# Four heads in 32-row tiles of TensorE, float32 numerators and two-bank tiles in the third stage of a four-stage kernel

## The chip, the cores and the metric

The kernel runs on one core of a Trainium2 chip. The metric is the device time of one execution in microseconds (us). The kernel has some 28,000 instructions on TensorE (PE), VectorE (DVE), ScalarE (ACT), GpSimd (POOL) and the DMA queues that SyncE (SP) issues.

## The reference, cut to what matters

Four sublayers follow one another on x of 2 x 1024 tokens of 128 features: an attention without a mask, a routed feed-forward network, a causal attention with linear position biases (the third stage, the one that is changed), and two layers of local attention with a feed-forward network. Each is added to x after a layer normalisation of its input and of its output. The third one:

```python
B, S, D, H = (2, 1024, 128, 16)            # S as x has it
HD = D // H                                # 8 features per head
q = (x @ Wq + bq).reshape(Bb, Ss, H, HD)   # k and v the same way
scores = jnp.einsum('bthd,bshd->bhts', q, k) / jnp.sqrt(jnp.asarray(HD, x.dtype))
alibi = slopes[:, None, None] * -jnp.abs(kpos - qpos)[None]
scores = scores + alibi[None]
scores = jnp.where(causal[None, None], -jnp.inf, scores)
attn = jax.nn.softmax(scores, axis=-1)
out = jnp.einsum('bhts,bshd->bthd', attn, v).reshape(Bb, Ss, Dd)
return out @ Wo + bo
```

## The kernel before, in words

**Stages.** The functions phase1 to phase4 are the four sublayers. A scheduler that simulates the engines orders the instructions of each engine, within what the data allow. Two things fix more than that. `in_line` (L129) chains the TensorE instructions of successive calls, so that PE executes them in the order of the program. And `tick` (L1541) lets the next stage prepare itself (load weights, make tables) behind instructions that are named to it.

**The third stage's units.** Two batches and four groups of four heads make eight groups (u = 0 to 7), of twelve steps each (`order`, L881). A step takes 128 keys (j) and a half of 512 queries (c): four steps for the first half, of widths 512, 384, 256 and 128, then eight for the second half, widths 512 four times without a mask and then 512, 384, 256, 128. A diagonal block is masked by one more matmul, the identity times a causal matrix in bfloat16 (L864, L897).

**q and k of a group (`make`, L821).** Both are kept as one stack of 128 rows in float16, so that a product of one pass has the precision of a split: rows 0 to 95 hold the 32 projected features (4 heads of 8) three times, as high part, low part and high part in the order that makes the wanted cross products; rows 96 to 127 hold constants for the position bias and, in q, the negated maximum of each query. A projection is 2 x 3 matmuls (`mm3`, L47, high and low parts); ACT evicts the high part, DVE subtracts for the low part, and a DMA brings the 32 constant rows. Since all four heads lie in the same 128 rows, k is spread into four copies `kz`, one per head, each with the other heads' rows multiplied by zero (four `tensor_scalar` of 128 x 1024; from the second group on two of them on POOL).

**Maxima (`max_pass`, L853, and `max_rows`, L871).** For each tile of 128 queries and each half of keys the products of all four heads are formed in PSUM, and DVE reduces them to negated maxima (L869). For four tiles at a time the maxima are transposed by four matmuls (L878) into rows 96 to 127 of q (copy L879 on ACT), so that the score product afterwards gives score minus maximum.

**Scores and values (`scores`, L883, and `values`, L906).** A product per head (L895), its mask (L897), and an exponent on ACT (L898) into float32 numerators `pt`. On even steps the numerators are split further into float16 high and low parts: a copy on ACT (L902) and a subtraction on POOL (L903), 128 x 4w each. Their product with the values (L920) accumulates in one PSUM bank, a column tile of 32 per head; on even steps it is float16 twice (low part, then high part), on odd steps once in float32.

**Output (`outputs`, L933, and `finish`, L952).** After each half of queries a matmul with a constant matrix (L942) brings the sums into token order, with normalisation on DVE. After a batch's last group the output projection and the layer normalisation follow.

**PSUM.** `bank` (L786) hands out single banks of 128 x 512 float32, alternately from two rings of three (`bankz` and `bank`); near the end only the latter is used, as the other is handed to the next stage. One unit of maxima or one product of 512 columns takes one bank.

**Order of the loop (L966 to L1003).** A step m issues in this order: the scores of step m, the pending update of the maximum rows, the values of step m-4, the maxima for the group that lies 12 steps ahead (38 reductions per group, spread over the steps), a projection of q or k for the next group in steps 3 and 5, and the outputs of step m-5. From m = 54 on each step ends with a tick for stage 4's preparation, which hangs on the newest exponent, reduction, DMA and `kz` product.

Of the kernel before, what the change touches and what calls it, by code (L numbers as in the profile page):

```python
# [22 lines left out]
NT = N // 128  # L23
# [681 lines left out]
def phase3(k, X):  # L705
# [5 lines left out]
    with ExitStack() as es:  # L711
# [10 lines left out]
        pick = cp.tile([128, 4], F32, name="pick")  # L722
        nc.sync.dma_start(pick, A["c_pick3"])
        both = cp.tile([128, G * (HD + 1)], F32, name="both")
        nc.sync.dma_start(both, A["c_both3"])
        bias = cp.tile([96, 2, G], F32, name="bias")
# [7 lines left out]
        for i, n in enumerate("qk"):  # L734
            w = work().rearrange("p t d -> p (t d)")[:, : G * 96].rearrange("p (g m) -> p g m", g=G)
            nc.sync.dma_start(w, A["t_wqk3"][:, i])
            h = cp.tile([128, G, 96], F32R, name=n + "wh")
            l = cp.tile([128, G, 96], F32R, name=n + "wl")
            if n == "q":
                nc.vector.tensor_scalar(w, w, scale, None, ALU.mult)  # L740
            k.split_r(h, l, w)
            wqk[n] = h, l
            yield
# [37 lines left out]
        pz = es.enter_context(k.psum("p3z", 3))  # L781
        pb = es.enter_context(k.psum("p3b", 3))
# [3 lines left out]
        def bank():  # L786

            turn[0] += 1
            other = turn[0] * 3 % 6 < 3 and not turn[1]
            return pz.tile([128, 512], F32, name="bankz") if other else pb.tile([128, 512], F32, name="bank")  # L790


        of = (vp, wp)
        V = [of[i].tile([128, NT, 16, HD + 1], F32, name=f"V{i}") for i in range(2)]

        V16 = [of[i].tile([128, NT, 16, 32], F16, name=f"W{i}") for i in range(2)]
        mx = wp.tile([128, G, NT, 32], F16, name="mx")
        nc.sync.dma_start(mx, A["c_mx3"])
        mx2 = wp.tile([128, 2, 4, 4], F16, name="mx2")
        ao = [k.acc, wp.tile([128, NT, D], F32, name="ao")]  # L800
        for i in range(2):
            nc.gpsimd.memset(V[i][:, :, :, HD : HD + 1], 1.0)
            nc.gpsimd.memset(V16[i][:, :, :, HD:32], 0.0)
            nc.gpsimd.memset(V16[i][:, :, :, HD : HD + 1], 1.0)

        def values_of(b):
            xTh, xTl = S["x", b]
            for c in range(2):
# [7 lines left out]
                v, h = V[b][:, 4 * c : 4 * c + 4, :, 0:HD], V16[b][:, 4 * c : 4 * c + 4]  # L816
                nc.scalar.copy(h[:, :, :, 0:HD], v)
                nc.gpsimd.tensor_tensor(h[:, :, :, HD + 1 : 2 * HD + 1], v, h[:, :, :, 0:HD], ALU.subtract)
                yield

        def make(u, n):  # L821
            b, g = u // G, u % G
            xTh, xTl = S["x", b]
            wh, wl = wqk[n]
            i = 0 if n == "q" else 1
            stk = qp.tile([128, N], F16, name=n + "st", bufs=3 if n == "q" else 1)
            S["dma"] = nc.sync.dma_start(stk[96:128, :], A["c_rows3"][i, g])
            bc = bias[:, i, g : g + 1]
            lo = slice(32, 64) if n == "q" else slice(64, 96)
            for c in range(2):  # L830
                s = slice(512 * c, 512 * c + 512)
                ps = bank()
                k.mm3(ps[:96, :], wh[:, g, :], wl[:, g, :], xTh[:, s], xTl[:, s])
                nc.scalar.activation(stk[:96, s], ps[:96, :], AF.Identity, bias=bc)
                nc.vector.scalar_tensor_tensor(stk[lo, s], ps[lo, :], bc[lo, :], stk[lo, s], ALU.add, ALU.subtract)
            if n == "k":
                kz = qp.tile([128, 4, N], F16, name="kz")
                for a in range(4):
                    if u and a < 2:
                        S["kz"] = nc.gpsimd.tensor_scalar(kz[:, a, :], stk, pick[:, a : a + 1], None, ALU.mult)  # L840
                    else:
                        nc.vector.tensor_scalar(kz[:, a, :], stk, pick[:, a : a + 1], None, ALU.mult)
                stk = kz
            S[n, u] = stk


        units = []
        for t in range(NT):
            for e in range(t // 4 + 1):
                m = {1: 4, 2: 2}.get(t + 1 - 4 * e, 1)  # L850
                units += [(t, e, a, m) for a in range(0, 4, m)]

        def max_pass(u, i):  # L853
            t, e, a0, m = units[i]
            n = 128 * min(4, t + 1 - 4 * e)
            ps = bank().rearrange("p (a n) -> p a n", a=m)
            q0, kz = S["q", u], S["k", u]
            diag = e == t // 4
            for a in range(m):
                nc.tensor.matmul(  # L860
                    ps[:, a, :n], q0[:, 128 * t : 128 * t + 128], kz[:, a0 + a, 512 * e : 512 * e + n], start=True, stop=not diag
                )
                if diag:
                    nc.tensor.matmul(ps[:, a, n - 128 : n], identb, causal[:, 0, :], start=False, stop=True)  # L864
            if e == 0:
                out = mx[:, u % G, t, :].rearrange("p (a r) -> p a r", r=8)[:, a0 : a0 + m, 6]
            else:
                out = mx2[:, u % 2, t - 4, a0 : a0 + m]
            S["max"] = nc.vector.tensor_reduce(out, ps[:, :, :n], AX.X, ALU.max, negate=True)  # L869

        def max_rows(u, c):  # L871
            if c:
                m = mx[:, u % G, 4:8, :].rearrange("p t (a r) -> p t a r", r=8)[:, :, :, 6]
                nc.vector.tensor_tensor(m, m, mx2[:, u % 2, :, :], ALU.min)
            ps = bank()
            for t in range(4 * c, 4 * c + 4):
                s = slice(128 * (t % 4), 128 * (t % 4) + 128)
                nc.tensor.matmul(ps[96:128, s], mx[:, u % G, t, :], k.ident16, start=True, stop=True, tile_position=(0, 96))  # L878
            nc.scalar.copy(S["q", u][96:128, 512 * c : 512 * c + 512], ps[96:128, :])  # L879
# [3 lines left out]
        def scores(n):  # L883
            u = n // 12
            c, j = order[n % 12]
            q1, kz = S["q", u], S["k", u]
            s = max(512 * c, 128 * j)
            w = 512 * c + 512 - s
            diag = j >= 4 * c
            pt = pp.tile([128, 4, 512], F32, name="pt")  # L890
            m = {128: 4, 256: 2}.get(w, 1)
            for a0 in range(0, 4, m):
                st = bank().rearrange("p (a n) -> p a n", a=m)
                for a in range(m):
                    nc.tensor.matmul(st[:, a, :w], kz[:, a0 + a, 128 * j : 128 * j + 128], q1[:, s : s + w], start=True, stop=not diag)  # L895
                    if diag:
                        nc.tensor.matmul(st[:, a, :128], identb, causal[:, 1, :], start=False, stop=True)  # L897
                S["exp"] = nc.scalar.activation(pt[:, a0 : a0 + m, :w], st[:, :, :w], AF.Exp)  # L898
            hl = None
            if n % 2 == 0:  # L900
                hl = pp.tile([128, 2, 4, 512], F16, name="hl", bufs=2)
                nc.scalar.copy(hl[:, 0, :, :w], pt[:, :, :w])  # L902
                nc.gpsimd.tensor_tensor(hl[:, 1, :, :w], pt[:, :, :w], hl[:, 0, :, :w], ALU.subtract)  # L903
            S["p", n] = pt, hl, s, w

        def values(n):  # L906
# [6 lines left out]
            pt, hl, s, w = S.pop(("p", n))  # L913

            parts = [(V[b], lambda a: pt[:, a, :w])]
            if hl is not None:
                parts = [(V16[b], lambda a, i=i: hl[:, i, a, :w]) for i in (1, 0)]
            for i, (v, of_head) in enumerate(parts):
                for a in reversed(range(4)):
                    nc.tensor.matmul(  # L920
                        po[32 * a : 32 * a + v.shape[3], s - 512 * c : 512],
                        v[:, j, 4 * g + a, :],
                        of_head(a),
                        start=j == 0 and i == 0,
                        stop=j == 4 * c + 3 and i == len(parts) - 1,
                        tile_position=(0, 32 * a),
                    )
# [5 lines left out]
        def outputs(n):  # L933
# [7 lines left out]
            for i in range(4):  # L941
                nc.tensor.matmul(ps[:, i, :, :], ot[:, 128 * i : 128 * i + 128], both, start=True, stop=True)  # L942
# [9 lines left out]
        def finish(b, c):  # L952
# [6 lines left out]
            ps = bank().rearrange("p (t d) -> p t d", d=D)  # L959
# [8 lines left out]
        todo = [(u, i) for u in range(groups) for i in range(len(units))]  # L968
        half = [t for t, *_ in units].index(4) - 1
        ahead = 12  # L970
        for n in "qk":
            make(0, n)
        done = 0
# [3 lines left out]
        for m in range(-ahead, steps + 8):  # L977
# [4 lines left out]
            turn[1] = int(m >= steps - 14)  # L982
            if 0 <= m < steps:
                put(scores, m)
            u = m + ahead
# [3 lines left out]
            rows = [(u // 12 - 1, 1)] if u % 12 == 0 and 12 <= u < steps + 12 else []  # L989
            if 0 <= m - 4 < steps:  # L990
                put(values, m - 4)
            while done < len(todo) and done < (u + 1) * len(units) / 12:
# [685 lines left out]
```

## Time and profile before

| what | value |
|---|---|
| runs | 1356.66, 1354.52, 1354.22 us (median 1354.52) |
| the profiled execution's own time | 1356.68 us |
| its span in the trace | 1354.9 us |
| granted TensorE clock, mean | 0.945 |
| stage 3: first projection, first scores, last scores, last output | 600.6, 640.9, 954.1, 980.4 us |
| reductions of the maxima on DVE, L869 (two groups) | 304 x 0.65 us, 198.7 us busy |
| exponents on ACT, L898 (two groups) | 304 x 0.58 us, 173.8 us busy |
| subtraction on POOL, L903 | 48 x 3.43 us, 164.4 us busy |

The page begins with the busy time of each engine over the whole span; those are means over four stages with different limits. A stretch view gives the same for parts of the span. The timeline of one engine has a line per run of equal instructions: start in us, duration of one (or, for several, of the run), engine, line, the program's names (output<-inputs), shapes, type and count. A wait stands behind in brackets with the engine and line that ended it. The other 1.8 us of the profiled execution lie around its span.

### The profile page before, as it was taken

How to read it: one execution, taken by the hardware profiler on the slowest of the kernel's cores; microseconds unless marked ns; L12 is line 12 of the kernel's file. 1: busy time of each engine (PE TensorE's matmuls, PEld its weight loads, DVE VectorE, ACT ScalarE, POOL GpSimd, SP SyncE). 2: the span in 40 equal slices, each digit the busy share in tenths (PEclk: the TensorE clock that was granted, in tenths of full speed). 3: DMA queues.
4: the chain of work that ended last, by engine and by line, in shares of the span. 5: the costliest groups of instructions: out<-in, count | busy, mean ns of one | idle time of the engine just before them, and what ended most of it. 6: DMA issues, size and time to landing. Idle time of an engine off the chain costs nothing.

```text
span 1354.9 us, 28455 instructions
## 1 busy us (share of the span) xinstructions
PE 1162.4 (86%) x11558; PEld 716.5 (53%) x11558; DVE 982.3 (72%) x1970; ACT 958.2 (71%) x1481; POOL 842.6 (62%) x525
## 2 busy tenths in 40 slices
PE   4799999999897889887799998798668898998886
PEld 1366666666565646443355544343336565666564
DVE  6777666776674385989888789571578887888855
ACT  2777777787686364541898987789367788887755
POOL 1666667777665463733676768785577886666611
PEclk8899999999898999998999999898679899999999
DMA  2000000000000031300000013000157666555520
GB/s 77 1 2 2 2 2 1 2 17 18 1 1 2 18 131 32 112 13 4 3 5 3 5 38 73 1 21 1 24 94 163 122 119 106 103 99 100 106 59 16
DMA packets 123394, 57.59 MB, mean 43 GB/s; under 512 B 105568, under 2 KB 114800, under 8 KB 123264
## 3 DMA queue, kind: packets, MB, share of 16 engines
q1 hardware_dynamic: 121360, 54.50, 18.7%
q8 instruction: 90, 1.47, 0.4%
q10 hardware_dynamic: 1472, 1.09, 0.3%
q0 software_dynamic: 432, 0.20, 0.2%
q14 instruction: 40, 0.33, 0.1%
HBM read 21.69 MB, written 1.11 MB: 17 GB/s over the span
## 4 chain that ended last, share of the span: by engine, by line
PE 42%; DVE 29%; ACT 14%; issue 6%; POOL 4%; DMA 3%; SPq 0%; POOLq 0%; DVEq 0%; ACTq 0%
DVE mx L869 5%; PE big L360 5%; PE pu L49 4%; PE pu L51 3%; PE pu L50 3%; DVE nm L332 3%; PE pu L920 3%; ACT pt L898 2%; PE big L49 2%; PE big L51 2%; PE big L50 2%; PE bank L895 1%; PE bank L860 1%; PE big L656 1%; DVE ln_st L81 1%
## 5 line engine op out<-in xcount | busy, mean ns | idle before, releaser
L367 POOL TENSOR_TENSOR hl<-p,hl 128x1024 f16<-128x1024 f32 x128 | 274.0, 2143 | 142.8 <-ACT hl L366 116.2
L903 POOL TENSOR_TENSOR hl<-pt,hl 128x2048 f16<-128x2048 f32 (+1 forms) x48 | 164.4, 3432 | 78.1 <-ACT hl L902 68.4
L332 DVE TENSOR_REDUCE nm<-big 128x2 f32<-128x1024 f32 x128 | 155.2, 1220 | 32.3 <-PE big L329 31.6
L364 ACT ACTIVATE p<-big 128x1024 f32<-128x1024 f32 x128 | 130.9, 1023 | 52.4 <-PE big L360 51.6
L49 PEld LDWEIGHTS <-hl 128*128 128x128 f16 x1024 | 100.5, 98 | 75.7 <-DVE acc L392 43.6
L366 ACT CAST hl<-p 128x1024 f16<-128x1024 f32 x128 | 133.8, 1045 | 4.1
L869 DVE TENSOR_REDUCE mx<-bank 128x1 f16<-128x512 f32 (+3 forms) x157 | 102.1, 653 | 32.1 <-PE bank L860 16.4
L869 DVE TENSOR_REDUCE mx<-bankz 128x1 f16<-128x512 f32 (+3 forms) x147 | 96.6, 660 | 18.7 <-PE bankz L864 12.8
L898 ACT ACTIVATE pt<-bank 128x512 f32<-128x512 f32 (+1 forms) x172 | 97.0, 582 | 18.5 <-PE bank L897 11.1
L49 PE MATMUL pu<-V1h,hl 128*128 128x129 f16 x512 | 92.6, 224 | 12.4 <-DVE acc L392 11.7
L49 PE MATMUL pu<-V0h,hl 128*128 128x129 f16 x512 | 93.1, 224 | 10.8 <-DVE acc L392 9.5
L50 PEld LDWEIGHTS <-hl 128*128 128x128 f16 x1024 | 101.3, 99 | 0.0
L1221 POOL TENSOR_TENSOR rot<-rot,rn 128x512 f32<-128x512 f32 x64 | 66.3, 1056 | 55.8 <-DVE rn L1211 50.4
L51 PEld LDWEIGHTS <-hl 128*128 128x128 f16 x1024 | 100.5, 98 | 0.0
L1196 POOL TENSOR_TENSOR rot<-rot,t 128x512 f32<-128x512 f32 x64 | 84.1, 1326 | 20.2 <-DVE t L1190 20.1
L51 PE MATMUL pu<-V0h,hl 128*128 128x129 f16 x512 | 92.5, 223 | 0.0
L50 PE MATMUL pu<-V0l,hl 128*128 128x129 f16 x512 | 92.5, 222 | 0.0
L51 PE MATMUL pu<-V1h,hl 128*128 128x129 f16 x512 | 92.0, 222 | 0.0
L50 PE MATMUL pu<-V1l,hl 128*128 128x129 f16 x512 | 92.0, 221 | 0.0
L898 ACT ACTIVATE pt<-bankz 128x512 f32<-128x512 f32 (+1 forms) x132 | 76.8, 583 | 20.8 <-PE bankz L897 9.9
L88 POOL TENSOR_TENSOR ln_rstd<-ln_rs,nhalf 128x4 f32<-128x4 f32 (+2 forms) x29 | 32.8, 1135 | 81.4 <-DVE ln_rs L84 67.3
L895 PE MATMUL bank<-qst,kz 128*128 128x512 f16 (+3 forms) x218 | 68.1, 345 | 13.5 <-DVE mx L869 7.5
(412 smaller groups left out, 3730.9 us busy)
## 6 DMA issues: line engine op xcount, KB each, us to landing
sb<-sd SPq DMA_DIRECT2D x16, 512.0 KB, 4.4
Vs<-V SPq DMA_DIRECT2D x60, 130.0 KB, 2.4
work<-in_t_w SPq DMA_DIRECT2D x2, 512.0 KB, 3.5
out<-F SPq DMA_DIRECT2D x3, 256.0 KB, 2.3
X<-in_L_attn_x SPq DMA_DIRECT2D x2, 256.0 KB, 3.3
w<-in_t_wqk SPq DMA_DIRECT2D x1, 512.0 KB, 5.1
wv<-in_t_wv ACTq DMA_DIRECT2D x1, 512.0 KB
X<-in_L_attn_x ACTq DMA_DIRECT2D x1, 512.0 KB, 5.0
```

The costliest lines, as they stand in the source:

```text
L49: mm(out, lh, rh, start=start, stop=False, **kw)
L50: mm(out, lh, rl, start=False, stop=False, **kw)
L51: mm(out, ll, rh, start=False, stop=stop, **kw)
L332: S["red"] = nc.vector.tensor_reduce(S["n", u][:, i // 2, c, :], ps, AX.X, ALU.max, negate=True)
L364: S["exp"] = nc.scalar.activation(p, st, AF.Exp, scale=QSCALE**-2)
L366: nc.scalar.copy(hl[:, 0], p)
L367: S["lo"] = nc.gpsimd.tensor_tensor(hl[:, 1], p, hl[:, 0], ALU.subtract)
L869: S["max"] = nc.vector.tensor_reduce(out, ps[:, :, :n], AX.X, ALU.max, negate=True)
L895: nc.tensor.matmul(st[:, a, :w], kz[:, a0 + a, 128 * j : 128 * j + 128], q1[:, s : s + w], start=True, stop=not diag)
L898: S["exp"] = nc.scalar.activation(pt[:, a0 : a0 + m, :w], st[:, :, :w], AF.Exp)
L903: nc.gpsimd.tensor_tensor(hl[:, 1, :, :w], pt[:, :, :w], hl[:, 0, :, :w], ALU.subtract)
L1196: eng("ra" if j else "rb", i).tensor_tensor(rot[:, j], rot[:, j], t2[:, j], ALU.add)
```

## The change

The four heads' rows no longer lie together by kind; each head's rows lie together in 32 partitions: its 8 features three times, then 8 rows of constants. The weights are laid out for that (t_wqk3 has 128 columns per group). `make` projects both halves into one two-bank tile, ACT copies the sum whole to float32 `t`, a multiplication with a column of zeros and ones (`low`) makes `hi`, a subtraction makes the stack (both on POOL, in the first group on DVE), and four DMAs, issued after that, bring each head's 8 constant rows. The spread `kz` and its products are gone.

`products` multiplies four heads: two per pair of banks, each from its own 32 rows (`tile_position`), followed by the masks of the two, full-height matmuls. The pairs come from one ring of three. A unit of maxima is now all four heads, two pairs and two reductions; there are 12 units per group, one per step. `max_rows` copies the whole half of q by a product with the identity, adds the maxima to it in four more matmuls, and copies the result back over q on ACT. The numerators are used in float32 in all steps; the copy L902, the subtraction L903 and the second values product are gone, and the float32 values are 32 wide. The loop keeps the maxima 10 steps ahead rather than 12, the values 2 steps late rather than 4 and the outputs 3 rather than 5; the update of the second half's rows comes in the step after its last maxima, where it came one step later.

```diff
-        pz = es.enter_context(k.psum("p3z", 3))
-        pb = es.enter_context(k.psum("p3b", 3))
+        pz = es.enter_context(k.psum("p3z", 1))
+        pb = es.enter_context(k.psum("p3b", 2))
...
+        def pair():
+            turn[0] += 1
+            if turn[0] % 3 == 1 and not turn[1]:
+                return pz.tile([128, 2, 512], F32, name="pairz")
+            return pb.tile([128, 2, 512], F32, name="pair")
...
         def make(u, n):
...
+            ps = pair()
             for c in range(2):
                 s = slice(512 * c, 512 * c + 512)
...
+                k.mm3(ps[:, c, :], wh[:, g, :], wl[:, g, :], xTh[:, s], xTl[:, s])
+            t = qp.tile([128, N], F32, name="t", bufs=2)
+            nc.scalar.activation(t, ps.rearrange("p c n -> p (c n)"), AF.Identity, bias=bias[:, i, g : g + 1])
+            hi = qp.tile([128, N], F16, name="hi", bufs=1)
+            stk = qp.tile([128, N], F16, name=n + "st")
+            eng = nc.gpsimd if u else nc.vector
+            eng.tensor_scalar(hi, t, low[:, i : i + 1], None, ALU.mult)
+            S["stk"] = eng.tensor_tensor(stk, t, hi, ALU.subtract)
+            for a in range(4):
+                S["dma"] = nc.sync.dma_start(stk[32 * a + 24 : 32 * a + 32, :], A["c_rows3"][i, g, a])
             S[n, u] = stk
...
+        row = lambda a: slice(32 * a, 32 * a + 32)
+        def products(l, r, w, mask=None, at=0):
+            for a0 in (0, 2):
+                ps = pair()
+                for e in range(2):
+                    d = row(a0 + e)
+                    nc.tensor.matmul(ps[:, e, :w], l[d, :], r[d, :], start=True, stop=mask is None, tile_position=(d.start, 0))
+                for e in range(2 if mask is not None else 0):
+                    nc.tensor.matmul(ps[:, e, at : at + 128], identb, mask, start=False, stop=True)
+                yield slice(a0, a0 + 2), ps[:, :, :w]
+        units = [(t, e) for t in range(NT) for e in range(t // 4 + 1)]
         def max_pass(u, i):
...
+            for a, ps in products(q0[:, 128 * t : 128 * t + 128], kst[:, 512 * e : 512 * e + n], n, mask, n - 128):
+                S["max"] = nc.vector.tensor_reduce(out[:, a], ps, AX.X, ALU.max, negate=True)
         def max_rows(u, c):
...
+            ps = pair()[:, 0, :]
+            q = S["q", u][:, 512 * c : 512 * c + 512]
+            nc.tensor.matmul(ps, k.ident16, q, start=True, stop=False)
+            for i in range(4):
+                nc.tensor.matmul(ps[:, 128 * i : 128 * i + 128], mx[u % 2][:, 4 * c + i, :], k.ident16, start=False, stop=i == 3)
+            nc.scalar.copy(q, ps)
         def scores(n):
...
+            for a, ps in products(kst[:, 128 * j : 128 * j + 128], q1[:, s : s + w], w, mask):
+                S["exp"] = nc.scalar.activation(pt[:, a, :w], ps, AF.Exp)
-                hl = pp.tile([128, 2, 4, 512], F16, name="hl", bufs=2)
-                nc.scalar.copy(hl[:, 0, :, :w], pt[:, :, :w])
-                nc.gpsimd.tensor_tensor(hl[:, 1, :, :w], pt[:, :, :w], hl[:, 0, :, :w], ALU.subtract)
         def values(n):
...
+            for a in reversed(range(4)):
+                nc.tensor.matmul(po[32 * a : 32 * a + 32, s - 512 * c : 512], V[b][:, j, 4 * g + a, :],
+                    pt[:, a, :w], start=j == 0, stop=j == 4 * c + 3, tile_position=(0, 32 * a))
...
+        ahead, lag = 10, 2
+        for m in range(-ahead, steps + lag + 4):
...
+            turn[1] = int(m >= steps - 8)
             if 0 <= m < steps:
                 put(scores, m)
             for unit in rows:
                 put(max_rows, *unit)
+            rows = []
+            if 0 <= m - lag < steps:
+                put(values, m - lag)
+            u, i = (m + ahead) // 12, (m + ahead) % 12
+            if u < groups:
+                put(max_pass, u, i)
+                if i in (half, 11):
+                    rows.append((u, int(i == 11)))
+                if i in (3, 5) and u + 1 < groups:
+                    put(make, u + 1, "q" if i == 3 else "k")
             ends[:] = [e for e in ends if put(next, e, 0) is None]
+            if 0 <= m - lag - 1 < steps:
+                put(outputs, m - lag - 1)
             if m >= 54:
+                k.tick(S["exp"], S["max"], S["dma"], S["stk"])
```

## The prediction, made before the changed kernel ran

> **What bounds it now.** I read the page's totals first, then the busy time in stretches, then the order of TensorE's work in one group of stage 3, then who waited in its slowest stretch.
>
> ```profile
> span 1354.9 us, 28455 instructions
> ...
> PE 1162.4 (86%) x11558; PEld 716.5 (53%) x11558; DVE 982.3 (72%) x1970; ACT 958.2 (71%) x1481; POOL 842.6 (62%) x525
> ```
>
> These are means over four stages, so I price the change in stage 3 alone. In the stretches (busy us and count of PE, PEld, DVE, ACT, POOL, then the granted clock, the DMA share and GB/s):
>
> ```profile
> 600.00:641.00 41.00, 27.95 (x141) 15.60 (x142) 38.76 (x94) 6.51 (x10) 14.84 (x9) 0.88 0.03 7
> ...
> 746.16:781.77 35.61, 33.95 (x294) 17.23 (x293) 27.72 (x50) 32.90 (x53) 26.15 (x9) 1.00 0.02 6
> ...
> 866.00:886.00 20.00, 13.55 (x96) 6.02 (x95) 7.67 (x15) 10.02 (x17) 19.92 (x11) 0.83 0.00 1
> ...
> 921.00:955.00 34.00, 28.68 (x197) 12.29 (x198) 1.42 (x6) 29.49 (x48) 18.36 (x5) 0.75 0.00 1
> 955.00:981.00 26.00, 13.19 (x78) 9.14 (x71) 17.59 (x52) 7.42 (x17) 12.61 (x18) 0.58 0.20 31
> ```
>
> Before 641 DVE is the limit. The second row is one undisturbed group of twelve steps: PE is 95% busy, ACT 92%. At 866 POOL never rests and PE starves; at 921, where no maxima are left, ACT leads. From TensorE's timeline the scores of step 0 of groups 0 to 7 begin at 640.9, 682.3, 719.7, 757.0, 794.4, 835.1, 884.9 and 920.9, and the last step at 954.1. Durations that I need (start, us):
>
> ```profile
> 750.49 0.22 PE L897 MATMUL bank<-causal,identb 128*128 128x128 bf16 x1
> 750.63 1.05 PE L920 MATMUL pu<-pt,V 128*9 128x512 f32 x8
> 751.62 0.34 PE L860 MATMUL bankz<-kz,qst 128*128 128x384 f16 x1
> ...
> 758.06 0.22 PE L897 MATMUL bank<-causal,identb 128*128 128x128 bf16 x1
> 758.21 0.61 PE L920 MATMUL pu<-hl,W 128*32 128x512 f16 x8
> 758.76 0.23 PE L860 MATMUL bankz<-kz,qst 128*128 128x128 f16 x1
> ```
>
> Start to start, float32 values of 512 columns hold PE for 0.99 us, the split ones for 0.55. A mask takes 0.055; the 0.15 from mask to values shows some 0.09 lost when the tiling changes. Stage 1 has the nearest thing to the new products, two 64-row tiles:
>
> ```profile
> 150.59 0.39 PE L360 MATMUL big<-qh,kh 64*128 64x512 f16 x2
> 150.82 0.38 PE L360 MATMUL big<-ql,kh 64*128 64x512 f16 x2
> ...
> 154.68 0.38 PE L329 MATMUL big<-kh,qh 64*128 64x512 f16 x2
> 154.99 0.23 PE L49 MATMUL pu<-V1h,hl 128*128 128x129 f16 x1
> ```
>
> Both of a pair pass in 0.21 to 0.23 us, the time of one; 0.31 at the change to 128 rows again shows about 0.1 for the switch. The large evictions are these:
>
> ```profile
> L332 DVE TENSOR_REDUCE nm<-big 128x2 f32<-128x1024 f32 x128 | 155.2, 1220 | 32.3 <-PE big L329 31.6
> L364 ACT ACTIVATE p<-big 128x1024 f32<-128x1024 f32 x128 | 130.9, 1023 | 52.4 <-PE big L360 51.6
> ```
>
> **TensorE's work does not shrink.** Per group, scores and maxima each have 4608 columns of four heads. Before: 72 x 0.217 = 15.6 us, 64 masks 3.5, values 4 x 0.55 + 2 x 0.34 + 2 x 0.99 + 2 x 0.76 + 2 x 0.34 = 7.1 and a switch into each 1.0, q and k 12 x 0.23 = 2.8, rows 0.6, outputs 2 x 0.87 = 1.7: 32.3 of the 35.6. After: 8 units without a mask at 0.5 (two pairs, a switch) 4.0; 16 with one, each twice a pair (mean 0.135), two masks 0.11 and two switches 0.2, 14.2; values all in float32 6 x 0.99 + 2 x 0.76 + 2 x 0.56 (between 384 and 128 columns) + 2 x 0.34 = 9.3; q and k 2.8; rows, now with a whole copy of q, 1.1; outputs 1.7: 33.1. What four heads side by side save, the switches around each mask and the float32 values take back. A 32-row tile is not in the trace; I take the 64-row row, with nothing saved by more than two at once, and the other bound is heads one after the other (rival 4).
>
> **The new ring.** Six single banks become three pairs, used in turn, each step taking two for scores (S1, S2) and two for maxima (M1, M2). So S2 of the next step needs M1's pair, which a 1.22 us reduction frees, and behind S2 in TensorE's order stand the values and the next M1. That loop is the least a step can take. Step 8: product to reduction 0.41, reduction 1.22, wait 0.05, S2 (384 columns, mask, switch) 0.37, values 1.07 with their switches: 3.12, where this trace has 3.50 (746.16 to 749.66). With masks the first term is 0.5 to 0.62; reductions of 768 and 512 elements I take as 0.95 and 0.69 (rows of 0.685 for 512). In step 1 the negated maxima must be complete before the row update, which now stands in the very next step and ahead of the values: 0.62 + 1.22 + 1.14 + 0.23 + 0.05 + 0.25 + 1.07 = 4.6, before 2.9. In step 5 q's projection takes a pair too, and the row update needs that pair, freed by a 1.1 us copy on ACT: 1.47 for S2's exponent, 1.38 projection, 1.3 copy with its waits, 0.5 update, 1.07 values: 5.75, before 4.3. The twelve, from step 0: 2.8, 4.6, 2.8, 2.1, 2.4, 5.75, 3.0, 4.3, 3.1, 2.65, 2.8, 2.6, sum 39.0; before 3.06, 2.9, 1.95, 2.99, 3.69, 4.27, 2.64, 3.24, 3.5, 3.01, 2.01, 2.35, sum 35.6. So **+3.4 us a group**.
>
> **What goes away.** ACT loses 48 copies (77.5 us), POOL 48 subtractions (164.6 us). In undisturbed groups that is beside PE and worth nothing. It counts here:
>
> ```profile
> 872.37 0.22 PE L897 MATMUL bankz<-causal,identb 128*128 128x128 bf16 x1
> 878.92 0.62 PE L920 MATMUL pu<-hl,W 128*32 128x512 f16 x4 [6.33 <-POOL hl L903]
> ...
> 869.69 4.95 POOL L1080 TENSOR_TENSOR tab<-tab,qs 128x512 f32<-128x512 f32 x4
> ```
>
> The numerators wait on POOL behind stage 4's tables. Afterwards POOL carries only the q and k splits (about 2.9 + 2.1 us each; nearest rows 2857 ns for the 1024-wide scaling and 2.14 for the subtraction) and the tables.
>
> **The sum**, us against before, stretch by stretch:
> - First scores: two 512-column units less before them (8 x 0.60 = 4.8 on DVE), group 1's split moved to POOL (4.7), against normalisation moved ahead (2.7) and a first product one later, as q and k now wait for whole-width copies, the split and then four DMAs (nearest row 1.8 us to landing): -6.
> - Group 0: 41.4 becomes 40: -1.4. Groups 1 to 4: +13.6.
> - Group 5: 49.8 becomes 41.4, without the POOL stall: -8.4. Group 6, without projections: 36.0 becomes 36.3.
> - Group 7: ten steps without maxima, ACT 1.9 where it had 1.9 and a 1.9 copy every other step: 33.2 becomes 28.5, -4.7.
> - After the last scores two or three sets of values remain, not five, and no output projection among them: -7.6.
> - Stage 4: the built order puts its first rotary products on DVE behind stage 3's last normalisation; before, item 0 was through by 962. +5 (0 to 10).
>
> Together -9. Later projections are hidden: k is wanted five steps, 18 us, after its projection ends, and copy, split and DMAs take some 11; if POOL or SP's queue were late there, every product behind it on PE would wait as long. The profiled run took 1356.7 us (span 1354.9), so 1347.5; the median shown is 2.2 lower, so **1345**.
>
> **Rivals.** (2) The ring does not bind, because exponents and reductions run ahead: groups of 33.1 plus the present 3.3 of stalls, 36.4. Then 2.6 less in seven groups: -27, **1327**. For it: ACT and DVE have less to do. (3) The clock falls and the change **loses**. PE now waits in nearly every step (33.1 of 39, 85%). The rows at 600 and 866, with PE 68% busy, show clocks of 0.88 and 0.83, the group at 95% shows 1.00. About 1.5 us of each loop are PE's; at 0.83 they cost 0.3 more, 3.7 a group: 42.7, seven times, +26 - 9 = +17, **1371**. It decides from groups of 40.3 on (39.0 + 9/7). [...] (4) The tiles do not run side by side: a mean 0.16 more in M1 and in S2, 3.8 a group, **1372**. Against it: the 64-row pairs above. (5) It comes out even.
>
> **How the numbers follow.** Forecast 0.35, rival 2 0.17, even 0.09, rival 3 0.32, rival 4 0.07. A measurement of this kernel can tell about 0.2% (2.7 us) from no change. So faster 0.52, same 0.09, slower 0.39. Ring latencies off by 0.3 us a step move seven groups by 25 us; the start of stage 4 and the first scores add 5 each: 1315 to 1378. Within the forecast alone, 1335 to 1352.
>
> **What would show it.** Right: PE waiting on DVE's reductions at the second score pair of most steps, groups near 39 us, no wait on POOL at the values, the last scores 18 us or more before the end of the output projection. Wrong: groups at 36 with PE never idle (rival 2); a clock below 0.9 in groups 1 to 4 (rival 3); starts of two row tiles a full matmul apart (rival 4). A stage 4 longer than now by over 10 us would be something I have not seen.

## The result, and the profile after

The changed kernel takes **1403.5 us** in the median (1391.4 to 1410.4), against 1355.1 us (1354.2 to 1356.7) before: a ratio of 1.035, 95% interval 1.027 to 1.042. It is slower; the prediction said 1345, with 1315 to 1378 as its range. The profiled execution took 1410.4 us. Its page, the totals and the row of granted clocks (40 slices of 35 us, tenths of full speed):

```profile
span 1407.6 us, 28151 instructions
...
PE 1213.6 (86%) x11574; PEld 710.0 (50%) x11574; DVE 948.1 (67%) x1812; ACT 873.6 (62%) x1301; POOL 706.9 (50%) x487
...
PEclk7999999999999999977986779957569999999998
```

ACT lost 85 us of work and POOL 136, as the change intends. PE gained 51 us of busy time with nearly the same number of matmuls (11,574 for 11,558). The last row says where: the clock drops in the slices from some 600 to 1060 us, which are stage 3 (to 1026.5) and the start of stage 4. The stretches of the prediction again, in the changed kernel (busy us and count of PE, PEld, DVE, ACT, POOL, granted clock, DMA share, GB/s):

```profile
600.00:641.00 41.00, 26.24 (x144) 14.72 (x142) 36.71 (x87) 6.87 (x7) 19.64 (x10) 0.72 0.03 7
641.00:921.00 280.00, 251.34 (x1816) 106.10 (x1814) 155.43 (x233) 140.45 (x192) 69.75 (x32) 0.83 0.06 14
921.00:955.00 34.00, 32.91 (x196) 12.09 (x195) 14.98 (x21) 15.36 (x21) 9.88 (x8) 0.55 0.13 34
955.00:981.00 26.00, 22.55 (x161) 8.62 (x160) 14.77 (x18) 13.14 (x25) 1.64 (x1) 0.71 0.00 1
```

From 641 on DVE, ACT and POOL are far from busy, PE is busy at 87 to 97%, and its clock is 0.83, later 0.55. In finer stretches there is no 0.83:

```profile
690.00:730.00 40.00, 37.47 (x308) 17.98 (x306) 25.24 (x38) 22.19 (x31) 9.95 (x4) 1.00 0.02 4
731.00:761.00 30.00, 29.28 (x152) 12.69 (x151) 10.61 (x16) 11.06 (x14) 4.96 (x2) 0.50 0.02 4
```

The clock is whole or half (1.0 or 0.5 in every clock record of this trace and of the one before), and it stays half for 30 us while PE is busy for 98% of them. A mean between is a mixture of the two. The evictions of the loop are as long as I took them (1024 elements: 1.22 us a reduction, 1.02 an exponent), and it is they that wait for PE (busy, mean ns of one, idle time before and what ended it):

```profile
L884 ACT ACTIVATE pt<-pair 128x1024 f32<-128x1024 f32 (+3 forms) x135 | 105.5, 803 | 119.1 <-PE pair L846 91.4
...
L859 DVE TENSOR_REDUCE mx<-pair 128x2 f16<-128x1024 f32 (+3 forms) x128 | 118.7, 946 | 83.9 <-PE pair L846 49.8
```

From the timeline of TensorE, the groups (from their step 0 to the next group's, in us, with the granted clock):

| group | 0 | 1 | 2 | 3 | 4 | 5 | 6 | 7 (11 steps) |
|---|---|---|---|---|---|---|---|---|
| before | 41.3 | 37.5 | 37.3 | 37.4 | 40.7 | 49.8 | 36.0 | 33.2 |
| forecast | 40 | 39.0 | 39.0 | 39.0 | 39.0 | 41.4 | 36.3 | 28.5 |
| after | 41.1 | 44.2 | 50.5 | 53.2 | 49.3 | 42.0 | 47.5 | 42.3 |
| clock after | 0.87 | 0.96 | 0.70 | 0.74 | 0.80 | 0.92 | 0.68 | 0.55 |

Against before, the first scores come 3.3 us earlier (637.6), the scores take 56.9 us more, from the last of them to stage 3's end it is 18.8 us instead of 26.3 (-7.5), and stage 4 takes 6.6 more: +52.7, which is the difference of the spans.

What precedes a fall? The clock fell at 686.2 us. PE's timeline around it (a wait stands in brackets, with what ended it), after one line of values at full clock:

```profile
660.17 1.06 PE L897 MATMUL pu<-pt,V 128*32 128x512 f32 x8
...
683.28 0.39 PE L844 MATMUL pair<-kst,qst 32*128 32x512 f16 x2 [0.22 <-DVE mx L859]
...
684.36 0.28 PE L844 MATMUL pair<-qst,kst 32*128 32x256 f16 x2
...
685.21 0.28 PE L844 MATMUL pair<-qst,kst 32*128 32x256 f16 x2 [0.34 <-DVE mx L859]
...
686.34 0.59 PE L868 MATMUL pairz<-qst,ident 128*128 128x512 f16 x1 [0.63 <-DVE mx L859]
...
687.28 1.93 PE L897 MATMUL pu<-pt,V 128*32 128x512 f32 x8
```

No wait is longer than 0.63 us, yet the eight values matmuls take 1.93 us instead of 1.06 right after. What is special is the work: narrow blocks in 32-row tiles.

Rows of 1 us tell when the clock changed:

```profile
686.00:687.00 1.00, 0.66 (x4) 0.39 (x4) 0.51 (x2) 0.34 (x1) 0.00 (x0) 0.59 0.00 0
730.00:731.00 1.00, 0.38 (x4) 0.20 (x4) 0.72 (x2) 0.55 (x1) 0.00 (x0) 0.78 0.00 0
```

A clock of 0.59 is whole for 0.18 us and half for 0.82, so it fell at 686.2; in the second row it fell at 730.6. In this trace such changes lie on a grid of 3.41 us (621.3, 631.6, 648.6, 686.2, 730.6: 3, 5, 11 and 13 steps apart; all 51 changes, and the 47 of the trace before, lie within 0.01 us of such a grid). For each step of this grid I added up the columns streamed (512 take 0.213 us at full clock, as 127 such matmuls in 27 us of clock_alone show) times the rows in use over 128, and divided by 3.41. Call it the weighted share; it is my estimate from the start times. The records don't say when within its time a matmul streams; placing it 0.1 us later moves a share by up to 0.04. In stage 3's scores every fall follows a share of 0.23 to 0.42, and of the grid steps that kept full speed the lowest has 0.37. At the half clock, where a column takes twice as long (0.42 us for 512, 111 in 47 us of clock_alone), it comes back after shares of 0.78 to 0.87 and after none of 0.77 or less (one of 0.94, at 1000 us, did not bring it back; I can't say why. It is mostly twelve float32 products of 128 columns that start 0.21 us apart, twice what 128 columns take at the half clock; counted by columns it has some 0.54). By these counts both limits are about the same amount of work per 3.41 us: 0.39 at full clock fills 0.78 at half. Weighted like this a group before has some 30 us of work in 37.4; after the change it has 17 to 23 in 42 to 53.

### The profile page after: what moved, and what is told of

Its sections match the earlier page's. It is cut to its first block, busy times and chain, and to the rows that moved or that the text cites. A ratio compares the mean times of both kernels' runs of the same rounds, so it can differ in the third digit from the quotient of the medians.

```text
span 1407.6 us, 28151 instructions
## 1 busy us (share of the span) xinstructions
PE 1213.6 (86%) x11574; PEld 710.0 (50%) x11574; DVE 948.1 (67%) x1812; ACT 873.6 (62%) x1301; POOL 706.9 (50%) x487
## 4 chain that ended last, share of the span: by engine, by line
PE 49%; DVE 29%; ACT 11%; issue 5%; DMA 3%; POOL 2%; SPq 0%; POOLq 0%; ACTq 0%; DVEq 0%
PE pu L897 6%; DVE mx L859 5%; PE big L360 5%; PE pu L49 4%; PE pair L844 4%; PE pu L51 3%; PE pu L50 3%; DVE nm L332 3%; PE pair L846 2%; PE pairz L844 2%; PE big L49 2%; DVE q L1209 2%; PE big L51 2%; PE big L50 1%; PE sm L919 1%
## 5 line engine op out<-in xcount | busy, mean ns | idle before, releaser
L884 ACT ACTIVATE pt<-pair 128x1024 f32<-128x1024 f32 (+3 forms) x135 | 105.5, 803 | 119.1 <-PE pair L846 91.4
L859 DVE TENSOR_REDUCE mx<-pair 128x2 f16<-128x1024 f32 (+3 forms) x128 | 118.7, 946 | 83.9 <-PE pair L846 49.8
L830 POOL TENSOR_SCALAR hi<-t,low 128x1024 f16<-128x1024 f32 x14 | 39.8, 2846 | 207.2 <-ACT t L825 207.1
L897 PE MATMUL pu<-pt,V 128*32 128x512 f32 (+3 forms) x768 | 105.7, 633 | 0.1
L859 DVE TENSOR_REDUCE mx<-pairz 128x2 f16<-128x1024 f32 (+3 forms) x64 | 62.5, 977 | 50.9 <-PE pairz L846 23.8
L1170 POOL TENSOR_TENSOR rot<-rot,t 128x512 f32<-128x512 f32 x64 | 83.4, 1314 | 17.5 <-DVE t L1164 17.3
L884 ACT ACTIVATE pt<-pairz 128x1024 f32<-128x1024 f32 (+3 forms) x57 | 47.0, 824 | 41.8 <-PE pairz L846 27.3
```

The source lines that it names most:

```text
L859: S["max"] = nc.vector.tensor_reduce(out[:, a], ps, AX.X, ALU.max, negate=True)
L884: S["exp"] = nc.scalar.activation(pt[:, a, :w], ps, AF.Exp)
L897: nc.tensor.matmul(po[32 * a : 32 * a + 32, s - 512 * c : 512], V[b][:, j, 4 * g + a, :], pt[:, a, :w], start=j == 0, stop=j == 4 * c + 3, ...
L1170: eng("ra" if j else "rb", i).tensor_tensor(rot[:, j], rot[:, j], t2[:, j], ALU.add)
```

## The experiments

The theories are named in the expectations: A, the clock follows the rows streamed; B, it follows the time in which PE has nothing; C, the ring of three pairs makes the groups long and the clock is a by-product. All ratios are to the kernel before, run on the same chip.

**1. clock_alone.** A kernel of its own on PE.

```python
tiles(1, 32, 140)    # one 32-row tile, 512 columns, 140 times; warm() = 64 full matmuls before each
tiles(2, 32, 140); rest(); tiles(2, 32, 140)
tiles(4, 32, 140); rest(); tiles(4, 32, 140)
columns(140)         # 128 rows, 32 columns
duty(1, 128, 24); duty(2, 128, 20); duty(3, 128, 18); duty(4, 128, 16); duty(4, 32, 16)
```

> A kernel of its own, which computes nothing of the reference (its output is x) and only runs TensorE in stretches of some 30 us, each after 14 us of matmuls of 128 rows: one 32-row tile without a pause; pairs of 32-row tiles; pairs again after 12 us of rest; four tiles side by side, and again after a rest; 32 columns of 128 rows; then bursts of 1, 2, 3 and 4 matmuls of 128 rows and of 4 with 32 rows, a reduction on VectorE of 0.68 us after each burst. Theory A: one tile (share 0.25) falls to the half clock; pairs (0.5) keep the full clock after the warm stretch and do not regain it after the rest, as 0.5 is below 0.78; four tiles (1.0) keep and regain it; 32 columns keep it; the bursts of 1 fall, of 2 (about 0.36) fall or are at the border, of 3 and 4 (over 0.45) keep it; bursts of 4 with 32 rows fall. Theory B: everything without a pause has and regains the full clock, and bursts of 4 behave alike with 32 and with 128 rows.

Its stretches (busy us and count of PE, PEld, DVE, POOL, granted clock, DMA share, GB/s): one tile; pairs; pairs after a rest; four tiles after a rest; 32 columns; bursts of 2, 3 and 4; bursts of 4 with 32 rows:

```profile
28.00:75.00 47.00, 47.00 (x111) 16.17 (x110) 0.00 (x0) 0.00 (x0) 0.50 0.00 0
96.00:123.00 27.00, 27.00 (x254) 11.96 (x252) 0.00 (x0) 0.00 (x0) 1.00 0.01 1
140.00:195.00 55.00, 55.00 (x260) 19.61 (x258) 0.00 (x0) 0.00 (x0) 0.50 0.00 1
...
264.00:288.00 24.00, 24.00 (x452) 10.96 (x448) 0.00 (x0) 0.00 (x0) 1.00 0.01 2
305.00:332.00 27.00, 27.00 (x127) 12.15 (x126) 0.00 (x0) 0.00 (x0) 1.00 0.00 1
...
404.00:427.00 23.00, 12.84 (x27) 3.21 (x26) 8.99 (x13) 0.00 (x0) 0.50 0.00 1
444.00:468.00 24.00, 12.11 (x45) 4.31 (x45) 10.54 (x16) 0.00 (x0) 1.00 0.00 1
485.00:512.00 27.00, 15.28 (x62) 5.74 (x60) 10.37 (x15) 0.00 (x0) 1.00 0.00 1
530.00:560.00 30.00, 21.40 (x47) 6.11 (x46) 7.61 (x11) 0.00 (x0) 0.50 0.00 0
```

All as A has it. PE without a pause gets half the clock with one 32-row tile (0.50, first row), and pairs never regain in 55 us (0.50) what they keep in the row above (1.00). What counts here is rows, not columns: 32 columns of 128 rows keep the clock (1.00, 32 rows of 128 columns have 0.50). Bursts of four keep it with 128 rows (1.00) and lose it with 32 (0.50), with the same pattern of waits. B is out. Four tiles do run side by side: 452 matmuls in 24 us, 0.21 us for four.

**2. and 3. fill_128_rows and fill_32_rows.** The same two matmuls at the same places, with 128 and with 32 rows.

```diff
+        def filler(rows):
+            ps = ps_sm.tile([128, 512], F32, name="sm")
+            for _ in range(2):
+                nc.tensor.matmul(ps, k.ident16[:rows], fill[:rows], start=True, stop=True, tile_position=(0, 0))
...
+            if 10 <= m < steps - 12 and m % 12 in (11, 0, 1):
+                put(filler, 128)    # 32 in fill_32_rows
```

> The changed kernel with two matmuls more (128 rows, 512 columns of float16, 0.21 us each, into a bank that nobody reads) at the end of steps 11, 0 and 1 of each group but the last, the steps in which the trace of the changed kernel shows the granted clock fall. Theory A (activity): the clock is set for each 3.41 us by the columns that TensorE streams, weighted by the rows in use; it halves when this is below some 0.38 of the time, and at the half clock it comes back from some 0.78. By A the granted clock of stage 3 goes from 0.8 to over 0.95, groups take 39 to 40 us and the kernel 1340 to 1360 us. Theory B (waits): what counts is how long TensorE has nothing in it, whatever the rows; B expects the same here. Theory C (the ring of three pairs alone makes the groups long, the clock is a by-product): 1405 to 1415 us, as 42 matmuls are added.

> The same matmuls at the same places with 32 rows instead of 128: the same time on TensorE, a quarter of the rows. Theory A: the weighted share rises by only 0.03, so the clock still falls in nearly every group, granted clock of stage 3 below 0.88, 1385 to 1415 us. Theory B: as with 128 rows, clock over 0.95, 1340 to 1360 us. Theory C: 1405 to 1415 us.

With 128 rows 1388.2 us (1.0255; 1.0219 to 1.0291), with 32 rows 1401.7 us (1.0363; 1.0335 to 1.0392). Groups 1 and 2 of the first and group 2 of the second, in stretches (columns as before):

```profile
681.00:725.00 44.00, 40.80 (x323) 17.78 (x320) 25.85 (x36) 23.28 (x32) 9.97 (x4) 0.96 0.02 4
725.00:767.00 42.00, 38.08 (x315) 16.77 (x314) 24.22 (x35) 22.53 (x30) 9.96 (x4) 1.00 0.02 4
```

```profile
722.00:770.00 48.00, 44.14 (x312) 18.78 (x310) 24.19 (x33) 22.61 (x30) 9.96 (x4) 0.79 0.02 4
```

More work made it faster, and only with all rows: A against B and C. But A's figure (1340 to 1360) is missed. With 32 rows it is 13.5 us slower, on the same chip. Groups 2 and 5 kept the clock and took 41.9 and 40.6 us; groups 1, 3, 4 and 6 lost it in steps that have no filler (2; 5 and 10; 7; 6). Two of these falls, in step 10 of group 3 and step 7 of group 4, came with waits of 4.05 and 2.74 us: a long wait lowers the share as well, as nothing streams in it.

**4. full_height_products.** The row tiles alone undone.

```diff
+            if n == "k":
+                kz = qp.tile([128, 4, N], F16, name="kz", bufs=2)
+                for a in range(4):
+                    (nc.gpsimd if u and a < 2 else nc.vector).tensor_scalar(kz[:, a, :], stk, sel[:, a : a + 1], None, ALU.mult)
...
-                    nc.tensor.matmul(ps[:, e, :w], l[d, :], r[d, :], start=True, stop=mask is None, tile_position=(d.start, 0))
+                    nc.tensor.matmul(ps[:, e, :w], l(a0 + e), r(a0 + e), start=True, stop=mask is None)
```

> The changed kernel with the row tiles alone undone: k is spread into four copies with zeros in the other heads' rows, and each product has all 128 rows; the ring of three pairs, the order, the float32 numerators stay. Two products of a pair now take 0.43 us where the two tiles took 0.22. Theory A: the weighted share is over 0.5 in every step, the clock stays above 0.95 in stage 3; groups of 40 to 42 us, 1350 to 1375 us. Theory B: the ring and its waits are the same, so the clock falls in most groups and the time is at or above that of the changed kernel, 1400 to 1430 us. Theory C: the loop is longer by two products of 0.21 us a step, 1405 to 1440 us.

1367.1 us (1.0104; 1.0072 to 1.0136): 36 us less than the changed kernel, though PE has more rows to stream and DVE and POOL have 18 and 19 instructions more. Group 2:

```profile
718.00:759.00 41.00, 37.20 (x292) 18.49 (x291) 23.76 (x31) 22.77 (x30) 15.19 (x7) 1.00 0.02 4
```

The clock is 0.99 from 641 to 921, undisturbed groups take 41.4 us. As A expected.

**5. float32_alone.** The other part alone, in the kernel before.

```diff
-        pp = pool("p3p", 4)
+        pp = pool("p3p", 5)
-        V = [of[i].tile([128, NT, 16, HD + 1], F32, name=f"V{i}") for i in range(2)]
+        V = [of[i].tile([128, NT, 16, 32], F32, name=f"V{i}") for i in range(2)]
-            if n % 2 == 0:
+            if False:
```

> One part alone: the kernel before with the numerators in float32 in all steps (a fifth buffer for them, as they are held until the values), all else as before: 128-row products, six single banks. Theory A (the clock follows the rows that TensorE streams): nothing lowers the share, the clock in groups 1 to 4 stays over 0.97. TensorE has 2.2 us a group more, of which the 3.3 us of stalls take a part: clean groups 36.5 to 37.8 us where they had 35.6 to 37.5; the stalls behind POOL in group 5 (8 to 11 us) and those of the last group go: 1338 to 1352 us. Rival: TensorE is the limit and every group pays all of the 2.2 us, with 8 back in group 5: 1360 to 1365 us.

**1324.9 us** (0.9787; 0.9772 to 0.9801): faster than both kernels, and than I expected. Group 2:

```profile
713.00:751.00 38.00, 36.46 (x304) 18.87 (x303) 29.07 (x56) 23.81 (x46) 5.96 (x2) 1.00 0.02 4
```

Undisturbed groups are 1 us longer (38.3), since PE carries float32 values (0.99 us for 512 columns of four heads, 0.55 split); but group 0 takes 37.1 (41.3 before), group 5 37.9 (49.8) and group 7 29.8 (33.2), at a clock of 0.94 (0.74).

**6. and 7. fill_all_steps and fill_all_and_finish.** The filler in every step (`if 0 <= m < steps - 1`); in the second also the output projection in the small bank.

```diff
-            ps = pair()[:, 0, :].rearrange("p (t d) -> p t d", d=D)
+            ps = ps_sm.tile([128, 4, D], F32, name="sm")
```

> The changed kernel with the two unread matmuls of 128 rows in every step. Theory A: the weighted share is over 0.45 in all windows of stage 3's groups, so the clock stays over 0.97 from the first full group on; groups of 40 to 42 us (the ring's loop, some of the 0.43 us a step hidden in its waits), and the two steps behind each output projection longer as before: 1355 to 1372 us. Theory C (the ring alone, the clock a by-product): 96 times 0.43 us more, 1430 to 1445 us.

> As fill_all_steps, and the output projection of finish goes into the small bank instead of one of the three pairs. In the trace of the changed kernel the projection holds a pair for some 7 us (matmuls, addition, layer normalisation), and step 10 of group 3 takes 6.35 us instead of 2.1, steps 5 to 7 of group 4 some 18 instead of 12.6. If the pair is what they wait for, 6 to 12 us less than fill_all_steps; if it is the vector work that is in the way of the reductions, the same within 2 us.

1411.5 us (1.0426; 1.0402 to 1.0450) and 1415.2 us (1.0459; 1.0423 to 1.0496). Both miss every expectation. The filler brought waits of its own for the small bank, 8.1 and 17.5 us by their sums, and the clock also fell behind such waits; in the second kernel it fell at 829.4, inside this one:

```profile
830.81 1.01 PE L803 MATMUL sm<-fill,ident 128*128 128x512 f16 x2 [4.86 <-DVE X L210]
```

Where nothing else used that bank (group 5) the clock was 1.00 and the group 43.3 us. Nothing follows on the projection from these two.

**8. single_banks.** The two-bank tiles alone undone, row tiles kept.

```diff
-            if turn[0] % 3 == 1 and not turn[1]:
-                return pz.tile([128, 2, 512], F32, name="pairz")
-            return pb.tile([128, 2, 512], F32, name="pair")
+            if turn[0] % 2 == 1 and not turn[1]:
+                return pz.tile([128, 1, 512], F32, name="bankz")
+            return pb.tile([128, 1, 512], F32, name="bank")
```

> The changed kernel with the two-bank tiles alone undone: two heads are still multiplied side by side in 32-row tiles, but into two single banks of a ring of six, each with its own reduction or exponent of 512 elements (0.68 and 0.6 us) instead of 1.22 and 1.02 for two. If the loop through the ring sets the pace, a bank is free some 0.5 us earlier: groups of 36 to 38 us at full clock; with the same work in less time the weighted share in steps 11 to 1 rises from some 0.38 to 0.42, at the border, so the clock falls less often: 1345 to 1385 us, granted clock of stage 3 over 0.88. If the ring is not what TensorE waits for: 1395 to 1410 us.

1389.0 us (1.0261; 1.0221 to 1.0301), clock 0.78 from 641 to 921. At full clock steps 0 and 8 are shorter (2.3 us each for 2.7 and 3.2) and step 9 is longer (3.9 for 3.0); step 6 takes 3.6 to 3.9 for 4.5, mostly at a clock of 0.84 to 0.89. But the clock fell in step 2 of five groups. Here the ring is worth less than the clock; with the clock held, experiment 10 prices it.

**9. and 10. full_height_finish and full_height_singles.** Experiment 4 with the projection in the small bank (the diff of 7), and experiment 4 with single banks (that of 8).

> As full_height_products (1367.1 us), and the output projection of finish is put into the small bank instead of one of the three pairs. There step 10 of group 3 took 7.7 us where others took 2.9, and steps 5 to 7 of group 4 18.5 where others took 13; in the trace of the changed kernel TensorE waits 4.05 us there for the addition that ends the layer normalisation. If it is the pair held by the projection: both go, and some 2 us at the end of the second batch, 1355 to 1361 us. If it is VectorE's work for the normalisation, which holds up the reductions: 1365 to 1369 us.

> As full_height_products, with six single banks in turn instead of three pairs, a reduction or exponent for each head, as before the change. What is left of the change is the new layout of q and k, their projection at full width, the float32 numerators and the shorter leads. If the ring of three pairs is what is left of the loss, its loop goes (groups of 41.4 us become 37.5 to 39) and the projection holds one bank of six: 1322 to 1345 us, near float32_alone (1324.9 us). If the layout or the leads cost something of their own: 1348 to 1367 us.

1359.4 us (1.0047; 1.0031 to 1.0062): 7.7 less. Step 10 of group 3 falls from 7.7 to 2.6 us, as expected; steps 5 to 7 of group 4 stay long (21.3). In the changed kernel the same wait, after the first projection:

```profile
815.99 1.06 PE L897 MATMUL pu<-pt,V 128*32 128x512 f32 x8
821.10 0.61 PE L844 MATMUL pairz<-kst,qst 32*128 32x512 f16 x2 [4.05 <-DVE X L210]
```

Single banks: 1340.7 us (0.9900; 0.9873 to 0.9926), 26 less than with pairs. Group 2 takes 38.3 us, as in float32_alone, but most others take 2 to 4 us more than there, and the time is 16 us above it.

**11. fill_into_sum.** Fillers that wait for nothing new: zero weights, added to the open sum of the values; and the projection in the small bank, as in 7.

```diff
+        def filler(count):
+            for _ in range(count):
+                nc.tensor.matmul(S["o"], zeros, fill, start=False, stop=False)
...
+            if lag <= m < steps and m % 12 == 1:
+                put(filler, 2)
...
+            if lag <= m < steps and m % 12 not in (5, 1):
+                put(filler, 2 if m % 12 in (11, 0, 2, 6, 7) else 1)
```

> The changed kernel, row tiles and pairs as they are, with 17 matmuls of 128 rows and 512 columns a group (1 or 2 in each step but one) whose weights are zero and which add to the open sum of the values, so that they wait for nothing new (in fill_all_steps they waited up to 4.9 us for the small bank); and the output projection in the small bank. Theory A (the clock follows the rows streamed): clock over 0.96 in groups 1 to 6, groups of 40 to 42 us, no step over 6 us: 1345 to 1365 us, so that row tiles at full clock come out about even with the kernel before. If the clock is not the cause: 1395 us and more.

1383.5 us (1.0214; 1.0164 to 1.0263): 20 less than the changed kernel, short of A's figure. The clock is 1.00 in groups 1, 2 and 5 and 0.75 in group 6; a clean group takes 42.3 us, fillers included. Fillers with zero weights kept the clock in these groups too.

**12. and 13. full_singles_late_rows and after_late_rows.** Experiment 10 and the changed kernel, with the maximum rows updated a step later.

```diff
-            rows = []
+            rows, soon = soon, []
...
-                    rows.append((u, int(i == 11)))
+                    soon.append((u, int(i == 11)))
```

The reason to try it is a wait in experiment 10. L874 is the addition of the maxima to the copy of q; PE's waits for it from 640 to 915 us (total, times, longest):

```profile
PE bank L874 <- DVE mx L869: 8.5, 6, 2.7
```

> As full_height_singles (1340.7 us), with both updates of the maximum rows one step later (steps 3 and 7 instead of 2 and 6; the scores need them at step 4 and in the next group). There TensorE waits 0.9 to 2.7 us for the addition to the maxima ahead of the update in step 2, 9.4 us in all, and step 2 takes 4.8 us. If this wait is what is left against float32_alone (1324.9 us): 1328 to 1334 us. If the projections at full width and the splits behind DMAs are: 1338 to 1343 us.

> The changed kernel with both updates of the maximum rows one step later, nothing else. The wait of 0.6 us and more ahead of the update in step 2 goes, and the stretch in which the clock fell in groups 1 to 6 (steps 11 to 2) has the same work in less time. Theory A: the weighted share there rises from some 0.38 to 0.42, at the border of what keeps the clock: fewer falls, 1375 to 1395 us, granted clock of the whole run 0.90 to 0.92. If the fall has nothing to do with that stretch: 1398 to 1408 us.

Experiment 10 with late rows: 1333.7 us (0.9860; 0.9843 to 0.9878), 7 us less. The changed kernel with late rows: 1406.3 us (1.0383; 1.0328 to 1.0439), no gain. The wait ahead of the update costs time at full clock, but isn't what starts the falls: group 1 kept the clock (42.1 us), but in groups 2, 3 and 6 it fell in steps 0 to 2 as before, and elsewhere in steps 5 to 7 and 10. My hope of 0.42 in place of 0.38 was too small a margin: in the changed kernel falls follow shares of up to 0.42.

**The ladder.** Each line adds one part:

| kernel | us | step |
|---|---|---|
| before (on these chips) | 1353 | |
| float32 numerators | 1324.9 | -28 |
| layout of q and k with its split, maxima in units of four heads, shorter leads | 1340.7 | +16 (7 of it the wait ahead of the rows) |
| two-bank pairs | 1367.1 | +26 (8 of it the pair held by the projection) |
| 32-row tiles: the changed kernel | 1403.5 | +36 |

The last line comes from another chip, where the kernel before takes 1355; by the ratios the step is +33, with an interval of some 11 us either way.

## Why the prediction was wrong

**The step that failed** is the clock, in the forecast and in the size of rival 3. The forecast kept full speed for the groups; that was an estimate of mine, and no run of the changed kernel shows it. What its trace shows in its place is a clock of 0.68 to 0.96 in groups 1 to 6. Rival 3 ("The clock falls and the change loses") named the right mechanism, but priced it at 0.83, "3.7 a group", and at seven groups of 42.7 us. The 0.83 was misread: it is a mean over a 20 us row in which the clock was whole and, from 877.1 to 883.9, half. Two rows beside it, at 921 and 955, already had 0.75 and 0.58. What was granted is the half (0.50 from 731 to 761), and in the shares counted above it came back after 0.78 and more. With half the clock all of PE's work takes up to twice as long (eight values matmuls 1.93 us for 1.06), not 1.5 us of a loop 20% longer: groups 1 to 4 and 6 took 44 to 53 us. And it was tied to the wrong cause. Rival 3 counted PE's busy time (85% of a group), but a 32-row pair has half of a full matmul's rows, and a mask streams only 128 columns. The weighted work of a group fell by a quarter to two fifths, which the section on TensorE's work did not see: its 32.3 and 33.1 us were times.

Short waits were no protection: the clock fell at 686.2 with no wait above 0.63 us, and the bursts of 2 in clock_alone, which each wait for a reduction of 0.69 us, ran at 0.50 from 404 to 427.

**The ring** was sized about right. At full clock the changed kernel's steps other than step 2 sum to 35.0 us (0, 1 and 3 to 11: 2.69, 2.98, 2.40, 2.48, 4.07, 4.49, 4.07, 3.16, 2.98, 2.08, 3.59), step 2 with the clock held took 4.76 in fill_128_rows: 39.7 against 39.0 forecast. In part that is luck, as single steps were off by up to 2 us: the waits ahead of the row updates came in steps 2 and 6 (4.76 and 4.49), where the sum had them in 1 and 5 (4.6 and 5.75, measured 2.98 and 4.07). The sign named for the ring was seldom seen: from 640 to 960 us PE waited for a reduction ahead of a pair 19 times, 8.4 us in all, not in most steps.

**The sum's groups** don't agree with its own sign. The +13.6 for groups 1 to 4 is four times 39.0 less 35.6, the sum of undisturbed steps. By the starts that the prediction lists, these groups lasted 37.4, 37.3, 37.4 and 40.7, so +13.6 means groups of 40.7 to 44.1, not the 39.0 that is named as the sign and stands in the table above; with 39.0 the sum would have come to some 1335. With the clock held group 2 took 41.9, fillers included (fill_128_rows).

**Missed**: the output projection as a holder of one of three pairs (4.05 us of waiting in group 3). It is 7.7 us at an undisturbed clock.

**Right**: POOL's stall in group 5 goes (42.0 us, forecast 41.4; the nearness is partly luck, as step 2 took 6.47 us at a clock of 0.57, for 4.76 with the clock held); the end (-7.5, forecast -7.6); the start of stage 4 (+6.6, forecast +5; its first rotary product on DVE now comes at 1027.8, behind stage 3's last normalisation); the first scores come earlier (-3.3, forecast -6). Pairs run side by side and a switch costs what was taken. A pair of 512 columns, its masks and the switches:

```profile
655.54 0.39 PE L844 MATMUL pairz<-kst,qst 32*128 32x512 f16 x2
655.86 0.28 PE L846 MATMUL pairz<-causal,identb 128*128 128x128 bf16 x2
656.08 0.39 PE L844 MATMUL pair<-kst,qst 32*128 32x512 f16 x2
```

0.54 us from pair to pair, where 0.21 + 0.11 + 0.2 was forecast. Rival 4 is out.

**Left open**: how long the change would take with the clock held. By the step sums a group would be 1.7 us shorter than with full-height products (41.4), so the clock costs more than the ladder's 36 us, by a rough estimate 36 + 8 x 1.7 = 50 of the 58 us by which the forecast was off; no run held it throughout. Nor do the runs give a sharp limit for the fall: the changed kernel's clock fell after shares of up to 0.42 and held after one of 0.37, and in clock_alone bursts of 3 held at some 0.40 (45 matmuls of 0.213 us in 24 us).

## What to carry to other kernels

Before cutting the rows of matmuls on a PE that waits, add up rows times columns per few microseconds, not busy time: below some 0.4 of a full stream the clock halved here (after shares of 0.23 to 0.42), and at half speed PE had to be filled to some 0.78 to get it back. A matmul "wasted" on zeros may be what holds the clock (0.99 from 641 to 921 in full_height_products, 0.83 with the row tiles). And take a change of several parts apart: one part of this one alone was 2.1% faster, and the rest cost 79 us.

## What the runs showed that I had not expected

PE can be busy without a pause and still get half the clock: 47 us of one 32-row tile at 0.50. Adding matmuls that nobody reads made the kernel some 15 us faster (fill_128_rows). The executions of the changed kernel spread over 19 us (1391 to 1410), those of the kernel before over 2.4 there and at most 7.5 on another chip; a share that lies near the limit is a possible reason, not tested.
